# Shared expert of a fused recurrent and mixture-of-experts kernel: a PSUM copy on ScalarE ahead of an addition, and one operand sum formed earlier

## The chip, the cores and the metric

The kernel runs on one core of a Trainium2 chip. The metric is the device time of one execution in microseconds (us); before the change the median of three runs was 2733.51 us, from 2730.9 to 2735.72 us. Five engines work beside each other, each through its own queue in order: TensorE (PE, with its weight loads as PEld), VectorE (DVE), ScalarE (ACT), GpSimd (POOL) and SyncE (SP), which issues most of the DMAs.

## What is computed

Two layers act on `x` (128 sequences, 64 steps, 512 features, all float32). The reference, cut to its core:

```python
# layer 0: GRU over the 64 steps, a ternary-weight linear layer, residual
r = sigmoid(i_r + h_r); z = sigmoid(i_z + h_z); n = tanh(i_n + r * h_n)
h = (1 - z) * n + z * h
x = x + (hs @ ternary(weight).T + bias)
# layer 1: depthwise causal convolution, then a mixture of 64 experts (top 6) and a shared expert
hidden = conv(x, cond) + b
routed = combine(silu(buf @ w_gate) * (buf @ w_up) @ w_down)      # 64 slots an expert
shared = silu(hidden @ sw_gate) * (hidden @ sw_up) @ sw_down      # 512 -> 704 -> 512
x = x + routed + shared
```

The change lies in the shared expert alone: `silu(hidden @ sw_gate) * (hidden @ sw_up) @ sw_down` for all 8192 rows.

## The kernel before

The program has four stages, one after the other: the GRU with its input products and linear layer (to 1500 us), the convolution, a stage of shared expert blocks beside routing (from 1530 us), and a stage of shared expert blocks beside the routed experts (from 2084 us). The rows of the shared expert are cut into 16 blocks `i` of four steps (512 rows). `shared(i)` is a generator; after each of its `yield`s the caller may record a piece of routing (`route`), of slot counting (`count_slots`) or of an expert pair (`expert_pair`). The order that results is then rearranged within each engine by a scheduler when the program is built, so the order on an engine is read from the built program, not from the code.

**Gate and up part.** The 704 columns are five chunks of 128 (and a rest of 64, multiplied together at L818). Each chunk `c` is one `Block`: the two halves of the contraction and gate and up form a 2 by 2 block product that is done with seven products instead of eight (Strassen-Winograd). Each product is two matmuls of 128 x 256 at L644, and it adds into one of four PSUM tiles: products 1 and 2 into `psx`, 6 into `y`, 7 and 4 into `psw`, 5 and 3 into `psz`. They are recorded in the order 1, 6, 7, 3 of the chunk before, 2, 4, 5. Since products 4, 2 and 3 add onto what stands in the PSUM tile of 7, 1 and 5, the tile has to be read between the two:

- product 1 is copied by ScalarE into `u2` (L672), and product 6 is added to it (L674);
- product 7 is read by VectorE, `u3 = ps + u2` (L677), and only then may product 4 write `psw`;
- product 5 is read by VectorE, `aT = ps + u3` (L679), and only then may product 3 of the chunk write `psz`; L680 multiplies by the gate;
- product 2 goes through Silu on ScalarE into `g1` (L683), product 4 is added to `u2` and goes through Silu into `g2` (L686, L687), product 3 gives the other half of `aT` (L689, L690).

**Operand sums.** The products need sums of the rows: `s1`, `s2`, `s4` in `space` (L810, L811, L837) and a difference in place (L836). For blocks 0 and 1 `space` is a tile of its own; for blocks 2 to 7 it is the storage of the rows of block `i - 2` (L798), whose results leave by DMA at L911; from block 8 on it is the tile `es`, of which there is one. The scheduler places L810 and L811 of block `i + 2` where the storage of block `i`'s rows comes free, which for blocks 2 to 5 is among the instructions of block `i`'s second `Down`: L810 overwrites the first of the four rows, L811 the second, each once that row's DMA (L911) has read it.

**Down part.** From block 2 on (`PLAIN = 2`) the product with `sw_down` is done by `Down`, twice a block (`p` = 0, 1), again as seven products, in the order 6, 1 | 7, 5 | 2, 4, a piece `v` | 3, pieces x, w, z, then the rest at L771. `Down.__init__` forms sums of `aT` into places 6 and 7 of `space` (L723, L724) and a difference in place (L725). `last_sum` (L729 to L732) forms `s4 = x12 - s2` in a tile named `g1`, the name that the Silu of product 2 uses too. Product 1 is copied into `u2` (L740) and product 6 added (L741); product 7 is read by VectorE into `u3` (L744); product 5 is read by VectorE into `v` (L747), and only then may product 3 add into `psz`. L791 adds up the result rows, and L911 (GpSimd's queue) sends them with accumulation into the output. `u3` has one buffer, `u2` two.

The names of a profile's tiles leave buffer numbers out: `u2`, `u3` stand as `u`, `g1`, `g2` as `g`.

Of the kernel before, what the change touches and what calls it, by code (L numbers as in the profile page):

```python
# [8 lines left out]
F32 = mybir.dt.float32  # L9
# [10 lines left out]
P = 128  # L20
# [22 lines left out]
def adaln_ffn_kernel(  # L43
# [22 lines left out]
    nc = tc.nc  # L66
# [88 lines left out]
    def conv_group(sl, g, ps):  # L155

        ps = ps.rearrange("p (j h t) -> p j h t", j=4, h=2)
        for j in range(4):
            i = nc.tensor.matmul(  # L159
                ps[:, j],  # L160
                xcs[sl % 2][:, :, g * 4 + j],
                tzs[sl % 2][:, :, g * 4 + j, :],
                start=True,
                stop=True,
            )
        grouped.append(i)
        return ps
# [5 lines left out]
    HK = KD // 2  # L173
# [3 lines left out]
    with (  # L177
# [106 lines left out]
        class Chunk:  # L284


            def __init__(self, t, c, ops):
                self.c, self.ops, self.ws = c, ops, wsum[c]
                self.g = [gip.tile([P, 2, HD], F32, name="gi") for _ in range(2)]
                gis[t, c], gis[t + 1, c] = (g.rearrange("p h d -> p (h d)") for g in self.g)  # L290
                self.ps = {}
# [149 lines left out]
        for t in range(T):  # L441
# [9 lines left out]
            for c in (0, 2, 1):  # L451
                ps = ps_gh.tile([P, D], F32, name=f"psgh{c}")
# [60 lines left out]
    def hid(t):  # L513
        return hids[t // TH][:, t % TH, :]
# [20 lines left out]
    with tc.tile_pool(name="ps_c", bufs=4, space=PSUM) as ps_c:  # L535
        for sl in range(NSL):
# [7 lines left out]
            for g in range(DS // 4):  # L544
                if early:
                    ps = early.pop(0)
                else:
                    ps = conv_group(sl, g, ps_c.tile([P, D], F32, name="psc"))
# [27 lines left out]
    sh = ctx.enter_context(tc.tile_pool(name="sh", bufs=1, side="right"))  # L576
# [43 lines left out]
    QT = NB // 2 * P  # L620
# [9 lines left out]
    def winograd(n, accs, lhs, rhs, k0=0):  # L630


        name = {1: "x", 2: "x", 6: "y", 7: "w", 4: "w", 5: "z", 3: "z"}[n]
        first = n in (1, 6, 7, 5)
        if first:
            accs[name] = (
                ps_y.tile([P, D], F32, name="y")
                if n == 6
                else ps_gu.tile([P, D], F32, name=f"ps{name}")
            )[:, :QT]  # L640
        ps = accs[name]
        for k in range(HK):
            r = rhs(k)
            nc.tensor.matmul(  # L644
                ps.rearrange("p (j b) -> p j b", b=P) if len(r.shape) == 3 else ps,
                lhs(k),
                r,
                start=(first and k == 0),
                stop=(k == HK - 1),
                skip_group_check=not first,  # L650
            )
        return ps

    add, mul = nc.vector.tensor_add, nc.vector.tensor_mul

    class Block:
# [5 lines left out]
        def product(self, n):  # L662
            ps = winograd(
                n,
                self.accs,
                lambda k: sws[n][:, k, self.c * P : (self.c + 1) * P],
                lambda k: self.ops[n][:, k],
            )
            one, two = self.aT[:, :QT], self.aT[:, QT:]
            if n == 1:  # L670
                self.u2 = shu.tile([P, QT], F32, name="u2")
                nc.scalar.copy(self.u2, ps)  # L672
            elif n == 6:
                add(self.u2, self.u2, ps)  # L674
            elif n == 7:
                self.u3 = sh.tile([P, QT], F32, name="u3")
                add(self.u3, ps, self.u2)  # L677
            elif n == 5:
                add(two, ps, self.u3)  # L679
                mul(two, two, self.g2)  # L680
            elif n == 2:
                self.g1 = sh.tile([P, QT], F32, name="g1")
                nc.scalar.activation(self.g1, ps, AF.Silu)  # L683
            elif n == 4:
                self.g2 = sh.tile([P, QT], F32, name="g2")
                add(self.g2, ps, self.u2)  # L686
                nc.scalar.activation(self.g2, self.g2, AF.Silu)  # L687
            elif n == 3:
                add(one, ps, self.u2)  # L689
                mul(one, one, self.g1)  # L690
# [20 lines left out]
    class Down:  # L711


        def __init__(self, p, aT, aTr, space):
            self.p, self.aT, self.aTr, self.accs = p, aT, aTr, {}
            self.steps = [slice(p * QT + j * P, p * QT + (j + 1) * P) for j in range(2)]
            s1, s2 = (
                space[:, (6 + n) * QT : (7 + n) * QT].rearrange("p (k b) -> p k b", k=HK)
                for n in range(2)
            )  # L720
            x11, x12 = (aT[:, h_ * HK : (h_ + 1) * HK, self.steps[0]] for h_ in range(2))
            x21, x22 = (aT[:, h_ * HK : (h_ + 1) * HK, self.steps[1]] for h_ in range(2))
            add(s1, x21, x22)  # L723
            nc.vector.tensor_sub(s2, s1, x11)  # L724
            nc.vector.tensor_sub(x21, x11, x21)  # L725
            self.x12 = x12
            self.ops = {1: x11, 2: x12, 4: x22, 5: s1, 6: s2, 7: x21}

        def last_sum(self):  # L729
            s4 = sh.tile([P, QT], F32, name="g1").rearrange("p (k b) -> p k b", k=HK)  # L730
            nc.vector.tensor_sub(s4, self.x12, self.ops[6])
            self.ops[3] = s4  # L732

        def product(self, n):
            ps = winograd(
                n, self.accs, lambda k: self.ops[n][:, k], lambda k: sds[n][:, k]
            )
            if n == 1:
                self.u2 = shu.tile([P, QT], F32, name="u2")
                nc.scalar.copy(self.u2, ps)  # L740
                add(self.u2, self.u2, self.accs["y"])  # L741
            elif n == 7:
                self.u3 = sh.tile([P, QT], F32, name="u3")
                add(self.u3, ps, self.u2)  # L744
            elif n == 5:
                self.v = sh.tile([P, QT], F32, name="g2")
                add(self.v, ps, self.u3)  # L747
# [45 lines left out]
    def sums_space(i):  # L793

        if i < PLAIN:
            return sh.tile([P, 3 * D], F32, name="space")
        if i < NI // 2:
            return rows_of(i - 2).rearrange("p j d -> p (j d)")  # L798
        return esp.tile([P, 4 * D], F32, name="es")

    def shared(i, sums=None):
# [3 lines left out]
        x11, x12 = rows[:, :HK, :2], rows[:, HK:, :2]  # L805
        x21, x22 = rows[:, :HK, 2:], rows[:, HK:, 2:]
        space = sums_space(i)
        s = space[:, : 3 * D].rearrange("p (n k j b) -> p n k j b", n=3, k=HK, j=2)
        s1, s2, s4 = s[:, 0], s[:, 1], s[:, 2]
# [48 lines left out]
        if i < PLAIN:  # L858
            for p in range(2):
                ys = [  # L860
                    ps_y.tile([P, D], F32, name="y")
                    if p == 0
                    else ps_gu.tile([P, D], F32, name=f"ps{'wz'[j]}")
                    for j in range(2)
                ]
                for cs in (range(full - 1), range(full - 1, full)):
                    for j in range(2):
                        for c in cs:
                            nc.tensor.matmul(
                                ys[j],  # L870
                                aT[:, c, p * QT + j * P : p * QT + (j + 1) * P],
                                swd[:, c, :],
                                start=(c == 0),
                                stop=False,
                            )
                        yield
                for j in range(2):
                    part = slice(j * rest, (j + 1) * rest)
                    nc.tensor.matmul(ys[j], aTr[part, p], swdr[part], start=False, stop=True)
                for j in range(2):  # L880
                    nc.scalar.copy(hid(i * NB + 2 * p + j), ys[j])
        else:
            for p in range(2):
                down = after
                down.product(6)
                down.product(1)
                yield
                down.last_sum()
                down.product(7)
                down.product(5)  # L890
                yield
                down.product(2)
                down.product(4)
                down.block("v")
                if p == 0:
                    after = Down(1, aT, aTr, space)
                yield
                down.product(3)
                for name in ("x", "w", "z"):
                    down.block(name)  # L900
                down.finish(rows_of(i), sums)
                if sums is not None:
                    for t in range(i * NB + 2 * p, i * NB + 2 * p + 2):
                        nc.sync.dma_start(out=out_t[t], in_=sums[:, t % NB])
                yield
# [463 lines left out]
```

## Time and profile before

| what | value |
|---|---|
| median of three runs | 2733.51 us |
| profiled execution, whole | 2733.45 us |
| its span, first to last instruction | 2731.6 us |
| granted TensorE clock, mean | 0.997 |
| busy in the span: VectorE / ScalarE / GpSimd | 1413.4 / 426.1 / 425.6 us |
| copy of product 1 on ScalarE (L672), 80 of them | 372 ns each |
| addition of product 7 on VectorE (L677), 80 of them | 424 ns each |
| the same in the down part (L744), 28 of them | 424 ns each |
| last sum of the down part (L731), 28 of them | 393 to 426 ns each |

TensorE's rows count four matmul records for a product, two passes for each of its two matmuls. Idle time in brackets in a timeline is the idle time of that engine just before the instruction, with what ended it. [...]

### The profile page before, as it was taken

How to read it: one execution, taken by the hardware profiler on the slowest of the kernel's cores; microseconds unless marked ns; L12 is line 12 of the kernel's file. 1: busy time of each engine (PE TensorE's matmuls, PEld its weight loads, DVE VectorE, ACT ScalarE, POOL GpSimd, SP SyncE). 2: the span in 40 equal slices, each digit the busy share in tenths (PEclk: the TensorE clock that was granted, in tenths of full speed). 3: DMA queues.
4: the chain of work that ended last, by engine and by line, in shares of the span. 5: the costliest groups of instructions: out<-in, count | busy, mean ns of one | idle time of the engine just before them, and what ended most of it. 6: DMA issues, size and time to landing. Idle time of an engine off the chain costs nothing.

```text
span 2731.6 us, 30112 instructions
## 1 busy us (share of the span) xinstructions
PE 2704.8 (99%) x11447; PEld 1866.4 (68%) x11447; DVE 1413.4 (52%) x3143; ACT 426.1 (16%) x794; POOL 425.6 (16%) x471
## 2 busy tenths in 40 slices
PE   8999999999999999999999999999999999999999
PEld 5666666666666666666679766777876656666667
DVE  6555555555555555555554655555664333433334
ACT  1111111111111111111110222222221111111111
POOL 2111111121111112111010000000001222222120
PEclk9999999999999999999999999999999999999999
DMA  5333221121111112311157641122256898998962
GB/s 189 92 77 79 73 66 51 43 54 55 47 51 43 50 43 54 77 47 51 35 140 218 216 137 21 37 58 58 63 150 186 272 323 247 314 316 260 284 180 47
DMA packets 329360, 327.98 MB, mean 120 GB/s; under 512 B 184384, under 2 KB 250432, under 8 KB 327040
## 3 DMA queue, kind: packets, MB, share of 16 engines
q1 hardware_dynamic: 302672, 255.52, 30.7%
q0 software_dynamic: 25984, 66.86, 10.6%
q10 hardware_dynamic: 560, 3.67, 0.6%
q8 instruction: 91, 1.49, 0.2%
q14 instruction: 53, 0.43, 0.1%
HBM read 239.73 MB, written 94.65 MB: 122 GB/s over the span
## 4 chain that ended last, share of the span: by engine, by line
PE 95%; DMA 2%; issue 2%; DVE 1%; ACT 0%; SPq 0%; DVEq 0%; POOLq 0%; ACTq 0%
PE psgh L454 24%; PE psw L644 7%; PE psz L644 6%; PE psx L644 6%; PE psw L308 6%; PE psz L308 6%; PE psx L308 6%; PE psf L387 4%; PE psc L159 4%; PE py L1274 3%; PE y L644 3%; PE psy L308 3%; PE pg L1250 3%; PE pu L1250 3%; PE y L818 2%
## 5 line engine op out<-in xcount | busy, mean ns | idle before, releaser
L454 PE MATMUL psgh<-whh,hT 128*128 128x512 f32 x1536 | 676.3, 596 | 0.7 <-ACT hT L369 0.7
L454 PEld LDWEIGHTS psgh<-whh,hT 128*128 128x128 f32 x1536 | 287.2, 190 | 351.3 <-issue 337.2
L308 PE MATMUL psx<-wih,xp 128*128 128x256 f32 x768 | 198.5, 381 | 6.5 <-DMA wih<-in_w_ih_dram 6.0
L197 POOL DMA_DIRECT2D xn<-in_x_dram x61 | 33.9, 556 | 845.0 <-DVE x L395 833.4
L308 PEld LDWEIGHTS psx<-wih,xp 128*128 128x128 f32 x768 | 143.7, 191 | 25.8 <-issue 6.0
L464 DVE TENSOR_TENSOR n<-psgh,bhn 128x512 f32<-128x512 f32 x64 | 44.2, 691 | 175.3 <-PE psgh L454 175.3
L369 ACT COPY hT<-psf 128x512 f32<-128x512 f32 x64 | 37.4, 585 | 584.0 <-PE psf L363 584.0
L461 DVE TENSOR_TENSOR r<-psgh,gi 128x512 f32<-128x512 f32 x64 | 44.2, 691 | 143.3 <-PE psgh L454 143.3
L159 PE MATMUL psc<-tz,xc 128*128 128x128 f32 x480 | 105.7, 383 | 0.0
L159 PEld LDWEIGHTS psc<-tz,xc 128*128 128x128 f32 x480 | 105.6, 313 | 0.0
L383 POOL TENSOR_TENSOR xn<-xn,fb 128x512 f32<-128x512 f32 x64 | 80.7, 1262 | 155.3 <-DMA xn<-in_x_dram 155.3
L308 PE MATMUL psz<-wih,xs 128*128 128x256 f32 x384 | 98.7, 379 | 1.8 <-DVE gi L331 1.8
L308 PE MATMUL psy<-t,xs 128*128 128x256 f32 x384 | 99.9, 383 | 0.3 <-DVE t L259 0.2
L308 PE MATMUL psw<-t,xp 128*128 128x256 f32 x384 | 98.8, 380 | 0.4 <-DVE u L329 0.4
L308 PE MATMUL psw<-wih,xp 128*128 128x256 f32 x384 | 98.7, 379 | 0.0
L308 PE MATMUL psz<-t,xs 128*128 128x256 f32 x384 | 98.7, 379 | 0.0
L387 PE MATMUL psf<-sgn,hhi 128*128 128x512 f32 x256 | 95.1, 493 | 0.0
L1274 PE MATMUL py<-wd,aeT 128*64 128x512 f32 (+1 forms) x384 | 90.6, 601 | 0.0
L1259 DVE SCALAR_TENSOR_TENSOR a<-a,rw,pu 128x352 f32<-128x352 f32 x32 | 18.6, 580 | 136.8 <-PE pu L1250 122.4
L323 DVE TENSOR_TENSOR p<-psx,bi 128x512 f32<-128x512 f32 x96 | 66.3, 691 | 37.5 <-PE psx L308 37.2
L644 PE MATMUL psx<-xr,swg 128*128 128x256 f32 x320 | 84.3, 385 | 0.0
L1284 POOL DMA_INDIRECT out_dram<-ys,idxp x32 | 45.4, 1418 | 249.9 <-ACT ys L1282 200.1
(298 smaller groups left out, 4687.2 us busy)
## 6 DMA issues: line engine op xcount, KB each, us to landing
wg<-in_w_gate_dram SPq DMA_DIRECT2D x64, 704.0 KB
wu<-in_w_up_dram SPq DMA_DIRECT2D x64, 704.0 KB
wd<-in_w_down_dram SPq DMA_DIRECT2D x64, 512.0 KB
x1c<-x SPq DMA_DIRECT2D x62, 256.0 KB
out_dram<-x SPq DMA_DIRECT2D x62, 256.0 KB
xn<-in_x_dram POOLq DMA_DIRECT2D x61, 256.0 KB
xp<-in_xT_dram POOLq DMA_DIRECT2D x30, 512.0 KB
tab<-hid SPq DMA_DIRECT2D x60, 256.0 KB
```

Of the source, the lines that this page charges most:

```text
L159: i = nc.tensor.matmul(ps[:, j], xcs[sl % 2][:, :, g * 4 + j], tzs[sl % 2][:, :, g * 4 + j, :], start=True, stop=True,)
L308: i = nc.tensor.matmul(ps, self.ops[n][:, k, :], self.ws[n][:, k, :], start=(first and k == 0), stop=(k == HK - 1), skip_group_check=not f ...
L323: add(self.p1, both, b)
L383: nc.gpsimd.tensor_add(xn, xn, fb)
L387: nc.tensor.matmul(ps, piece[:, k, :], sgn[:, k, :], start=(i == 0 and k == 0), stop=(i == 1 and k == KD - 1),)
L454: nc.tensor.matmul(ps, hT[:, k, :], whh[c][:, k, :], start=(k == 0), stop=(k == KD - 1))
L461: nc.vector.tensor_add(r, ps_r, gis.pop((t, 0)))
L644: nc.tensor.matmul(ps.rearrange("p (j b) -> p j b", b=P) if len(r.shape) == 3 else ps, lhs(k), r, start=(first and k == 0), stop=(k == HK ...
L818: nc.tensor.matmul(gu.rearrange("p (j b) -> p j b", b=P), swr[:, k].rearrange("p w n -> p (w n)"), rows[:, k], start=(k == 0), stop=(k == ...
L1250: nc.tensor.matmul(acc[halves[j]], xeT[:, k, halves[j]], ws[j][which][:, k, :], start=(k == 0), stop=(k == KD - 1),)
L1274: nc.tensor.matmul(py[halves[j]], aeT[:n, c, halves[j]], ws[j][2][:n, c, :], start=(c == 0), stop=(c == len(ech) - 1),)
L1284: nc.gpsimd.indirect_dma_start(out=out, out_offset=bass.IndirectOffsetOnAxis(ap=(idxp[:CAP] if j == 0 else idxo)[:, q : q + 1], axis=0), i ...
```

## The change

Two things are changed. Product 7, in `Block` and in `Down`, is copied out of PSUM by ScalarE into `u3`, and VectorE then adds `u2` in place. And `Down` forms its last sum `s4` in its `__init__`, after the other three, in place `p` of `space` (the first two places, which held the row sums `s1`); the method `last_sum` and its tile named `g1` are gone.

```diff
             elif n == 7:
                 self.u3 = sh.tile([P, QT], F32, name="u3")
-                add(self.u3, ps, self.u2)
+                nc.scalar.copy(self.u3, ps)
+                add(self.u3, self.u3, self.u2)
...
             nc.vector.tensor_sub(x21, x11, x21)
-            self.x12 = x12
-            self.ops = {1: x11, 2: x12, 4: x22, 5: s1, 6: s2, 7: x21}
-
-        def last_sum(self):
-            s4 = sh.tile([P, QT], F32, name="g1").rearrange("p (k b) -> p k b", k=HK)
-            nc.vector.tensor_sub(s4, self.x12, self.ops[6])
-            self.ops[3] = s4
+            s4 = space[:, p * QT : (p + 1) * QT].rearrange("p (k b) -> p k b", k=HK)
+            nc.vector.tensor_sub(s4, x12, s2)
+            self.ops = {1: x11, 2: x12, 3: s4, 4: x22, 5: s1, 6: s2, 7: x21}
...
             elif n == 7:
                 self.u3 = sh.tile([P, QT], F32, name="u3")
-                add(self.u3, ps, self.u2)
+                nc.scalar.copy(self.u3, ps)
+                add(self.u3, self.u3, self.u2)
...
                 down.product(6)
                 down.product(1)
                 yield
-                down.last_sum()
                 down.product(7)
                 down.product(5)
```

## The prediction

> **What bounds the kernel now.** The page comes first: TensorE is busy for 99% of the span and makes up 95% of the chain that ended last, so an edit on VectorE or ScalarE counts only where TensorE waits for them.
>
> ```profile
> PE 2704.8 (99%) x11447; PEld 1866.4 (68%) x11447; DVE 1413.4 (52%) x3143; ACT 426.1 (16%) x794; POOL 425.6 (16%) x471
> PE 95%; DMA 2%; issue 2%; DVE 1%; ACT 0%; SPq 0%; DVEq 0%; POOLq 0%; ACTq 0%
> ```
>
> Second, TensorE's waits from 1530 us on, the stages with the shared expert (total, times, longest): 4.7 us for product 7's addition L677, which frees `psw`, and 1.2 us for L747, which frees `psz` in the down part.
>
> ```profile
> PE psw L644 <- DVE u L677: 4.7, 7, 0.8
> PE psz L644 <- DVE st L613: 1.4, 1, 1.4
> PE psz L644 <- DVE g L747: 1.2, 4, 0.4
> PE psz L644 <- DVE aT L689: 0.5, 1, 0.5
> ```
>
> Third, the timeline at one such wait, the first chunk of block 3. Product 7 was through by 1726.9, but L677 stood behind L837 (held by a DMA), L928, two pairs of L831 and L674, and ran at 1728.59. Product 4, due at 1727.22 + 4 x 0.216 = 1728.08, began at 1729.07: 0.99 us lost.
>
> ```profile
> 1725.28 0.38 ACT L829 ACTIVATE g<-y 64x256 f32<-64x256 f32 x1
> 1725.57 0.69 DVE L837 TENSOR_TENSOR hid<-hid 128x512 f32<-128x512 f32 x1 [2.64 <-DMA out_dram<-hid]
> 1725.68 0.37 ACT L672 COPY u<-psx 128x256 f32<-128x256 f32 x1
> 1725.92 1.03 PE L644 MATMUL psw<-hid,swu 128*128 128x256 f32 x4
> ...
> 1727.22 1.03 PE L644 MATMUL psx<-hid,swg 128*128 128x256 f32 x4
> ...
> 1727.56 0.38 ACT L829 ACTIVATE g<-y 64x256 f32<-64x256 f32 x1 [1.50 <-DVE aTr L831]
> ...
> 1728.59 0.42 DVE L677 TENSOR_TENSOR u<-psw,u 128x256 f32<-128x256 f32 x1
> ...
> 1729.07 0.48 PE L644 MATMUL psw<-hid,st 128*128 128x256 f32 x1 [0.82 <-DVE u L677]
> ```
>
> Fourth, VectorE at the end of block 2, the second `Down`. L810 waits for one output row's DMA, L747 follows it, L811 waits for the next row's.
>
> ```profile
> 1715.72 0.69 DVE L810 TENSOR_TENSOR hid<-hid 128x512 f32<-128x512 f32 x1 [1.72 <-DMA out_dram<-hid]
> 1716.33 0.42 DVE L747 TENSOR_TENSOR g<-psz,u 128x256 f32<-128x256 f32 x1
> 1717.87 0.69 DVE L811 TENSOR_TENSOR hid<-hid 128x512 f32<-128x512 f32 x1 [1.13 <-DMA out_dram<-hid]
> ```
>
> Both programs were also built and their order on each engine compared. TensorE keeps its instructions, with as many changes from one line to another (929) and nearly its order; VectorE keeps its counts; ScalarE gains 108 copies. VectorE's order changes in two repeated places, which decide the forecast (after's instructions under before's line numbers):
>
> ```
> end of blocks 2 to 5, before: L741, L744, L810, L747, L811, L791
> end of blocks 2 to 5, after:  L741, L810, L744, L811, L747, L791
> first Down of blocks 2 to 15: L731 before: after L690;  after: ahead of L679
> ```
>
> **Part 1, the copy on ScalarE.** 108 copies (80 + 28) at 372 ns (the rows of L672 and L740) are 40 us on an engine busy for 16%; VectorE's addition stays. What it can remove are the L677 waits. Counted like the 0.99 above they are 0.68 and 0.66 (blocks 1, 2), 0.99, 0.95, 0.89, 0.88 (blocks 3 to 6) and 0.85 (block 8): 5.9 us, the upper bound. The lower bound is 0, if the copy itself is late. In the built order the copy stands behind the second L829. In block 3 that starts at 1727.56; the copy follows 0.40 later (as L672 follows L829 at 1725.28 above), takes 0.37 and ends at 1728.33. With 0.05 for the release and 0.1 for a weight load no longer hidden (a group after a stall lasts 1.13 instead of 1.03) product 4 starts at 1728.48, so 0.6 of 0.99 is won; blocks 4 to 6 repeat it: 2.4. In blocks 1 and 2 L829 lies earlier (1603.41, copy done at 1604.18, product 4 due at 1604.24): all 1.34. In block 8 VectorE is held by gathered rows (L1235) on the next steps too, so I take 0.4 of 0.85. Together -4.1 us.
>
> `u3` has one buffer, so the copy now also waits for the previous chunk's L679. That ran at 1731.10 in block 3, and the next product 7 at 1733.07: covered. Behind the copy on ScalarE stand the two Silus, which wait for later products anyway.
>
> [...] This trace has 424 ns for L677, with a PSUM operand, and 425 ns for L690, with none. [...]
>
> **Part 2, the last sum earlier.** Removed is one instruction of 0.42 us after L690, where no wait of TensorE hangs on it. Added is the same one ahead of L679 in the first `Down` of 14 blocks, because its new place held `s1` and product 5 reads that last. L679 frees `psz` for product 3, and has little room:
>
> ```profile
> 2157.69 0.42 DVE L679 TENSOR_TENSOR aT<-psz,u 128x256 f32<-128x256 f32 x1
> ...
> 2158.25 1.05 PE L644 MATMUL psz<-es,swu 128*128 128x256 f32 x4
> ```
>
> Here (block 9) L679 would run from 2158.03 (+0.34, the distance of two such additions), end at 2158.45 and let product 3 start at 2158.60: 0.35 lost. The same sum gives 0.24 to 0.35 in blocks 7 to 12, 14 and 15 and nothing in 13 (a piece of expert work lies between): 2.3 us. In blocks 2 to 6 two instructions (L731, L959) now stand ahead, but one product matmul (0.43) was moved ahead of product 3: 0.15 each, 0.7. Sum +3.0; bounds 0 (if VectorE starts the sum earlier) and 14 x 0.35 = 4.9.
>
> From block 9 on the next block's L810 must wait for the second `Down`'s product 3, which now reads `es`. In block 8 that product ends at 2081.5; L810, L811 and L837, 0.72 apart as now, keep VectorE until 2083.6, and L791 behind them, which waits for TensorE's last matmuls, was due at 2083.5: almost hidden. I take +0.3 for all seven; without that cover 7 x 0.7 = 5.
>
> **Part 3, what both do to VectorE's order.** Now L747 stands behind L811. L811 cannot start before its DMA has landed, 1717.87 in block 2; L747 follows 0.61 later (L747 after L810 above), ends at 1718.90, and product 3 starts at 1718.95 instead of 1716.80: 2.15 us. Blocks 3, 4, 5, with L811 at 1779.83, 1841.02, 1903.06 and product 3 at 1778.49, 1840.30, 1901.84: 2.42, 1.80, 2.30. Sum +8.7. The DMA was issued after L791 of the first `Down`, before the stall, so its landing does not move; what follows (L791, the next rows' DMAs, L837) moves along with TensorE and gives nothing back. Bounds: 5.7 if that DMA landed 0.75 sooner each time, 11.7 if as much later.
>
> Block 0 has its sums L614 to L616 behind routing work; about 0.4 of new waits, from -0.3 to 1.
>
> **Sum.** -4.1 + 3.0 + 0.3 + 8.7 + 0.4 = +8.3 us on the profiled execution's 2733.45 (span 2731.6 and 1.85 around it; the median is 2733.51): 2741.8 us, 0.3% slower. No change means within 0.2%, 5.5 us, about what a measurement of this kernel can tell.
>
> **Rivals.** (a) Nearly balanced: the copy wins the whole 5.9, the early sum costs half, 1.5, and L811's DMA lands sooner: 2733.45 - 5.9 + 1.5 + 5.7 = 2734.8. For it: the L677 waits are there in every block. Against: the second L829 holds ScalarE. (b) Faster: L811's wait does not reach TensorE, because its DMA lands by 1715.9 instead of 1717.8, that is right after L810's row. This is one place, the second `Down` of blocks 2 to 5; from there on the copy's 4.1, plus the 1.9 of L747's present waits if L810 too comes early, stand against 3.7: 2731.2 us, and faster by over 5.5 needs the early sum hidden and the copy's whole 5.9 as well, 2726.4. Against: the two rows landed 1.8 to 2.4 us apart all four times. (c) Slower still: beside the experts the copy queues on ScalarE behind a copy of expert results (L1282) that waits for `py` or an output DMA; `psw` is then late where it never was. At 1 us for one chunk in five of 35, +7: 2749. For it: in the built order L1282 stands directly ahead of some copies, and waited 2.4 us for a DMA once. Against: TensorE's order puts those matmuls first too. (d) The change does not do what it says: excluded, the built order has the copies and the moved sum.
>
> **How the numbers follow.** Forecast 0.66, with its own range 2738 to 2746; (a) 0.17, (b) 0.06, (c) 0.11. Slower by over 0.2% (2739.0): 0.62 of the forecast and (c), 0.73. Within: the rest of the forecast, (a) and half of (b), 0.24. Faster: 0.03. The range reaches down into (a) and up to (c): 2735 to 2748.
>
> **What would show it.** In the profile after: L747 right behind L811 at the end of blocks 2 to 5, and TensorE's wait on L747 near 8 to 10 us instead of 1.2; the wait on L677 gone and one on the copy of some 1.5 us in its place; a wait on L679 of about 2 us in the later blocks. The forecast is wrong if L747's wait stays near 1 us, or if TensorE waits for ScalarE beside the experts.

## The result, and the profile after

The changed kernel takes 2743.21 us (median of six runs, 2741.28 to 2745.92) against 2731.86 us for the kernel before (six runs beside them, 2730.84 to 2735.72): a ratio of 1.0040, 95% interval 1.0027 to 1.0053. The profiled execution has a span of 2742.0 us, 10.4 more than the one of before.

Work moved as the code says. The page's first line of the changed kernel has 108 more instructions and 40 us more on ScalarE; VectorE has as many instructions as before (3143) and 1412.1 us instead of 1413.4:

```profile
PE 2708.1 (99%) x11447; PEld 1869.6 (68%) x11447; DVE 1412.1 (51%) x3143; ACT 466.4 (17%) x902; POOL 425.9 (16%) x471
```

Line numbers in the changed kernel: the copy of product 7 is L678 and its addition L679; product 5's addition L681; in the down part copy L743 and addition L744; the early sum L730; L747, L810, L811 are as before. TensorE's waits from 1530 us on (total, times, longest):

```profile
PE psz L644 <- DVE g L747: 9.7, 4, 2.5
PE psz L644 <- DVE st L613: 3.2, 1, 3.2
PE y L644 <- DVE es L726: 1.2, 1, 1.2
PE psz L644 <- DVE aT L691: 0.6, 1, 0.6
```

The line of L677 with 4.7 us is gone, the one of L747 has gone from 1.2 to 9.7 us, and no line names L681, the addition that the early sum stands ahead of. Counted as in the prediction (start of a matmul less the time it was due), L747 costs 10.39 us in four places instead of 1.89. The timeline at the first of them, the end of block 2:

```profile
1712.13 0.69 DVE L810 TENSOR_TENSOR hid<-hid 128x512 f32<-128x512 f32 x1 [2.40 <-DMA out_dram<-hid]
1712.15 0.59 PE L754 MATMUL y<-swd,aT 128*128 128x256 f32 x2
1712.74 0.42 DVE L744 TENSOR_TENSOR u<-u,u 128x256 f32<-128x256 f32 x1
1714.13 0.69 DVE L811 TENSOR_TENSOR hid<-hid 128x512 f32<-128x512 f32 x1 [0.98 <-DMA out_dram<-hid]
1714.74 0.42 DVE L747 TENSOR_TENSOR g<-psz,u 128x256 f32<-128x256 f32 x1
...
1715.21 2.07 PE L644 MATMUL psz<-swd,hid 128*128 128x256 f32 x4 [2.46 <-DVE g L747]
...
1717.08 1.06 PE L754 MATMUL psx<-swd,aT 128*128 128x256 f32 x2
```

L747 stands behind L811 and its DMA, as forecast. But the last two rows hold something that was not: the product takes 2.07 us instead of 1.03 and the piece behind it 1.06 instead of 0.59. The windows of the same stretch (busy time of PE, PEld, DVE, ACT, POOL with instructions, then the granted TensorE clock, DMA share and GB/s) show what goes with it:

```profile
1711.82:1715.23 3.41, 0.94 (x6) 0.49 (x4) 2.05 (x4) 0.00 (x0) 0.00 (x0) 1.00 0.38 65
1715.23:1718.64 3.41, 3.41 (x8) 2.78 (x9) 0.00 (x0) 0.00 (x0) 0.00 (x0) 0.50 0.00 0
1718.64:1722.05 3.41, 3.41 (x15) 1.80 (x15) 1.15 (x3) 0.37 (x1) 0.69 (x2) 1.00 0.00 0
```

After the stall the clock was granted at half for 3.41 us. The trace of the changed kernel has such a stretch of 3.41 us at 0.50 behind each of the four stalls (from 1715.23, 1780.08, 1844.93 and 1909.78 us) and one in block 8 (from 2073.63); the kernel before has none from 1532.97 us to its last microsecond. Measured from one L818 to the next, blocks 2 to 5 are 3.0 to 3.5 us longer each, block 8 is 1.4 longer, block 6 is 0.65 shorter, blocks 1 and 7 change by -0.5 and +0.2, and blocks 9 to 15 are the same to 0.01 us (the last to 0.11).

Two theories stood after this. A: the loss is the order of L811 and L747, plus a half-clock stretch behind each stall; the early sum is free. B: the prediction's sum, with the half clock unrelated to the stalls. It was also open which of the two edits brings the order.

### The profile page after: what moved, and what is told of

The parts are those of the page before. It is cut to its first block, busy times and chain, and to the rows that moved or that the text cites. A ratio compares the mean times of both kernels' runs of the same rounds, so it can differ in the third digit from the quotient of the medians.

```text
span 2742.0 us, 30320 instructions
## 1 busy us (share of the span) xinstructions
PE 2708.1 (99%) x11447; PEld 1869.6 (68%) x11447; DVE 1412.1 (51%) x3143; ACT 466.4 (17%) x902; POOL 425.9 (16%) x471
## 3 DMA queue, kind: packets, MB, share of 16 engines
q0 software_dynamic: 25984, 66.86, 10.4%
## 5 line engine op out<-in xcount | busy, mean ns | idle before, releaser
L467 ACT ACTIVATE n<-n 128x512 f32<-128x512 f32 x64 | 40.3, 629 | 274.0 <-DVE n L466 274.0
L644 PE MATMUL psx<-hid,swg 128*128 128x256 f32 x320 | 84.1, 385 | 0.7 <-ACT g L685 0.4
```

What stands on the lines that cost most here:

```text
L467: nc.scalar.activation(n, n, AF.Tanh)
L644: nc.tensor.matmul(ps.rearrange("p (j b) -> p j b", b=P) if len(r.shape) == 3 else ps, lhs(k), r, start=(first and k == 0), stop=(k == HK ...
```

## The experiments

Every kernel was timed in five rounds against the kernel before, whose medians in the three groups of runs were 2731.70, 2730.45 and 2730.66 us.

### One edit at a time

**The copy alone** (the kernel before with only the first hunks of the change).

> Kernel before with product 7 copied out by ScalarE in both classes; the down part's last sum stays after L690. VectorE's order at the end of blocks 2 to 5 is then that of the changed kernel: L741, L810, copy's addition, L811, L747, although the sum was not moved. Theory A (the copy alone brings the order; the stalls on L747 cost 8.5 us and each is followed by 3.41 us of TensorE at a granted clock of 0.5, some 1.65 us more): before 2731.9 - 4.7 (waits of product 7 gone) + 8.5 + 4 x 1.65 = 2742.3 us, wait on L747 near 10 us, four or more rows of clock 0.5. Rival B (the prediction's sum: no clock, the early sum costs 3): 2731.9 - 4.1 + 8.7 = 2736.5 us, and the missing rest with the sum. Rival C (the order comes from both edits together): 2731.9 - 4.5 = 2727.4 us, wait on L747 near 1.2 us.

Measured 2743.41 us, ratio 1.0036 (1.0023 to 1.0050): the whole loss without the moved sum. In its waits L747 is L749 (first line); the last of the four stalls is followed by half clock (0.50 from 1913.79 to 1917.20 us), and the mean granted clock is 0.996.

```profile
PE psz L644 <- DVE g L749: 9.9, 4, 3.3
```

**The early sum alone.**

```diff
 # changed kernel, in Block and in Down
-                nc.scalar.copy(self.u3, ps)
-                add(self.u3, self.u3, self.u2)
+                add(self.u3, ps, self.u2)
```

> Changed kernel with product 7's sum read from PSUM by VectorE again, as before; only the down part's last sum is early. VectorE's order at the end of blocks 2 to 5 is then that of the kernel before (L747 between L810 and L811). Theory A (the early sum takes the place of two copies of gathered rows, L1235, that go behind, and costs TensorE nothing in blocks 9 to 15; in block 8 the down part's sums wait for es, up to 1.2 + 1.65 us): 2731.9 + 0 to 3 us, 2732 to 2735, with blocks 9 to 15 as long as before to 0.1 us each. Rival B (the prediction: the early sum delays product 3 by 0.24 to 0.35 us in each late block, hidden in the changed kernel only because the copy made VectorE's product 7 work shorter): 2731.9 + 3.0 = 2735, spread over blocks 7 to 15.

Measured 2731.22 us, ratio 1.0001 (0.9992 to 1.0010); blocks 9 to 15 differ from before by no more than 0.05 us each, block 8 is 0.14 longer, and blocks 2 to 5 are 0.2 to 0.5 shorter (the waits on product 7's addition fell from 4.7 to 3.4 us; no run tells why). The sum costs nothing there with or without the copy, so rival B is out.

**The copy in the gate and up part only, and in the down part only.** Each has one of the two hunks with the copy.

> Kernel before with the copy on ScalarE in the 80 products of the gate and up part only; the down part keeps its addition from PSUM and its late sum. VectorE's order at the end of blocks 2 to 5 stays that of before (L810, L747, L811). Theory A (the waits of product 7 are all in the gate and up part; the loss comes with the down part's copy, which puts L744 one ScalarE step later and so lets L810 and L811 in ahead): 2731.9 - 4.7 = 2727.2 us, wait on L747 near 1.2 us. Rival B (the copy in either class moves the sums): 2737 us or more.

Measured 2727.00 us, ratio 0.9989 (0.9980 to 0.9998).

> Kernel before with the copy on ScalarE in the 28 products of the down part only. Theory A (the whole loss comes with this copy): VectorE's order at the end of blocks 2 to 5 is L741, L810, L744, L811, L747; the waits on L677 stay (5.9 us), the stalls on L747 rise by 8.5 us and bring four stretches of half clock: 2731.5 + 8.5 + 4 x 1.65 = 2746.6 us. Rival B (the order costs only together with the gate and up part's copy): 2732 us.

Measured 2747.07 us, ratio 1.0053 (1.0040 to 1.0067). Its waits show both the stalls on L747 (here L748) and the ones that the other copy would remove:

```profile
PE psz L644 <- DVE g L748: 10.1, 4, 3.2
PE psw L644 <- DVE u L677: 4.0, 7, 0.7
```

Its order at the end of block 2 is L741, L810, L744, L811, L747, that of the changed kernel; in the kernel with the 80 copies alone L744 and L747 stand where they stood before. Theory A had half clock behind all four stalls; the trace has 0.50 from 1853.06 to 1856.47 us, but 1.00 behind the last stall (the last section has the windows), and the five runs spread from 2742.5 to 2749.0 us, so that the hit on 2746.6 is no proof of the sum.

So 80 copies gain, and the 28 of the down part lose all that is lost. That they bring the order is shown by these two runs; the reason is argued from the code: they make L744 ready one ScalarE instruction later, and the order that is built for this has room for L810 and L811 ahead of L744 and L747.

### The order undone

```diff
 # changed kernel; v_sums keeps each L747, the addition of product 5 in Down
-        nc.vector.tensor_add(s1, x21, x22)
-        nc.vector.tensor_sub(s2, s1, x11)
+        held = 2 * PLAIN <= i < NI // 2
+        with tc.issue_after(v_sums[2 * (i - 2 - PLAIN) + 1].ins) if held else nullcontext():
+            nc.vector.tensor_add(s1, x21, x22)
+            nc.vector.tensor_sub(s2, s1, x11)
```

> Changed kernel, with the two sums L810 and L811 of the block after next put behind L747 in VectorE's queue (an issue order, four times); nothing else moves. Theory A (order plus clock): the stalls of 10.4 us on L747 go, and with them the four stretches of 3.41 us at clock 0.5: after 2743.2 - 10.4 - 6.6 = 2726 us, no granted clock under 1 in blocks 2 to 5. Rival B (the half clock is not tied to these stalls): 2743.2 - 10.4 = 2733 us, with four or five rows of clock 0.5 left between 1700 and 2080 us. Rival C (the sums are late where they now stand, and hold the next block's work): 2738 or more, with a wait of TensorE for L810 or L791 instead.

Measured 2726.15 us, ratio 0.9979 (0.9970 to 0.9989): 17.1 us less than the changed kernel, for four issue orders. The end of block 2 now (L747 is L748, L810 and L811 are L813 and L814):

```profile
1712.12 0.42 DVE L748 TENSOR_TENSOR g<-psz,u 128x256 f32<-128x256 f32 x1
...
1713.23 0.69 DVE L813 TENSOR_TENSOR hid<-hid 128x512 f32<-128x512 f32 x1 [0.69 <-DMA out_dram<-hid]
...
1714.00 1.03 PE L644 MATMUL psz<-swd,hid 128*128 128x256 f32 x4
...
1715.96 0.69 DVE L814 TENSOR_TENSOR hid<-hid 128x512 f32<-128x512 f32 x1 [2.04 <-DMA out_dram<-hid]
1716.25 0.48 PE L772 MATMUL psx<-swdr,aTr 64*128 64x256 f32 x1
```

L814 still waits for its DMA (2.04 us), but nothing that TensorE needs stands behind it: product 3 takes 1.03 us instead of 2.07. The mean granted clock is 0.999 instead of 0.997, which leaves room for two stretches of 3.41 us at half in the whole program, not for four (an estimate from mean and span: 2 x (1 - 0.9985) x 2724.2 = 8.2 us). Blocks 2 to 5 together are 18.5 us shorter than in the changed kernel's profile. The stalls were 10.4 of them. Half rate over 3.41 us, with TensorE busy for 3.41 of them (1715.23 to 1718.64 above), loses 1.7, and four such stretches 6.8; product 4 is late by 0.2 us there instead of 1.0, which is another 0.8; 0.5 stays unassigned. (The whole profiles differ by 17.8 us: block 8 is 1.3 shorter, about the 1.4 by which it had grown, and block 1 starts 2.1 later.)

> Copy on ScalarE alone, and L810, L811 behind L747 as in the run before this one; the last sum stays after L690. Theory A: before 2731.9 - 4.7 (product 7's waits) - 1.2 to 1.9 (what L747 waited for L810 before) = 2725 to 2726 us, faster than both kernels; if the early sum is free, within 2 us of the run with both edits and the order undone. Rival B (the copy only helps where something else stalls behind it): 2730 us or more.

Measured 2725.94 us, ratio 0.9980 (0.9970 to 0.9989), the same as with the early sum. Both versions beat both kernels, by 0.2% the kernel before.

### How long a stall brings the half clock

Two kernels were to make stalls of chosen length with additional VectorE instructions ahead of L747 (7 and 10 times, blocks 2 to 5).

```diff
             elif n == 5:
+                for _ in range(self.extra):
+                    nc.vector.tensor_tensor(self.u3, self.u3, self.u3, ALU.max)
                 self.v = sh.tile([P, QT], F32, name="g2")
```

> The copy kernel with L747's order undone (median 2725.9), and at the end of blocks 2 to 5 seven additional VectorE instructions on product 7's sum, each the maximum of it with itself, ahead of the addition of product 5. VectorE reaches that addition 7 x 0.40 - 1.5 (the time it had to spare in that place) = 1.3 us late, four times. [...] Rival B (any stall of over 1 us brings the half clock): 2725.9 + 4 x (1.3 + 1.65) = 2737.7 us, with four rows of 0.5.

Measured 2729.42 us, ratio 1.0001 (0.9991 to 1.0010).

> The same kernel with ten such instructions, so that the stall is 10 x 0.40 - 1.5 = 2.5 us, as long as those of the changed kernel, without any wait for a transfer and without the early sum. Theory A (idle length alone brings the half clock): 2725.9 + 4 x (2.5 + 1.65) = 2742.5 us with three or four stretches of 3.41 us at 0.5, each right behind a stall. Rival B (the half clock comes with the order of the two sums or with the transfers they wait for): 2725.9 + 4 x 2.5 = 2735.9 us and no row of 0.5 there.

Measured 2731.72 us, ratio 1.0005 (0.9996 to 1.0014). Neither tells anything of the clock, because the stalls did not come about: TensorE's order was built anew around the known VectorE work, with the next groups ahead of product 3. In the second of the two (L747 is L753) even the next block's L826 went ahead of it:

```profile
1716.03 0.59 PE L777 MATMUL psw<-swdr,aTr 64*128 64x256 f32 x2
1716.55 1.13 PE L826 MATMUL y<-hid,swr 128*128 128x512 f32 x2
1717.72 1.13 PE L644 MATMUL psz<-swd,g 128*128 128x256 f32 x4
```

TensorE waited 0.2 us here instead of 2.5. Blocks 2 to 6 together are still 4.0 and 5.3 us longer in these profiles than in the kernel that they started from; how much of that is the regrouped order was not settled. So these two runs leave open whether the half clock comes with the idle time or with the order of the sums and their transfers; the half clock that the kernel before has in its GRU stage, in the last section, speaks to that.

The third try used the real wait, a transfer: only L811 (here L814) is put behind L747 (L748), L810 (L812) stays ahead of L744 (L745).

> Changed kernel with only the second of the two sums, L811, put behind L747; L810 stays where it is, ahead of copy's addition L744. VectorE then waits for the first row's transfer alone, so L744 runs at the time it has in the changed kernel (1712.74 us in block 2) and L747 0.4 later: TensorE's stall is some 1.1 us instead of 2.6, four times. [...] Rival B (any stall of about 1 us brings 3.41 us of half clock): 2726.2 + 4 x (1.1 + 1.65) = 2737 us, with rows of 0.5 behind them.

Measured 2731.04 us, ratio 1.0004 (0.9995 to 1.0013); 2726.15 and four stalls of 1.1 us, without any half clock, make 2730.6. The end of block 2:

```profile
1713.62 0.69 DVE L812 TENSOR_TENSOR hid<-hid 128x512 f32<-128x512 f32 x1 [2.20 <-DMA out_dram<-hid]
...
1714.23 0.42 DVE L745 TENSOR_TENSOR u<-u,u 128x256 f32<-128x256 f32 x1
1714.75 0.42 DVE L748 TENSOR_TENSOR g<-psz,u 128x256 f32<-128x256 f32 x1
...
1715.23 1.13 PE L644 MATMUL psz<-swd,hid 128*128 128x256 f32 x4 [0.79 <-DVE g L748]
```

Its four stalls are 0.96, 1.41, 0.93 and 0.95 us, 4.25 in all; blocks 2 to 5 are 4.9 us longer than in the kernel without them (the medians, of two groups of runs, are 4.9 apart as well). The product behind the first stall takes 1.13 us, not 2.07, the clock behind the longest is 1.00, and the mean over the profile is 0.999. So these four cost 4.9 us for 4.25 us of stalls, while the four of the changed kernel cost their 10.39 us and, by the half clock, 6.8 more. The window with the longest of these stalls, and the one behind it:

```profile
1773.51:1776.92 3.41, 2.36 (x11) 1.72 (x10) 1.31 (x3) 0.00 (x0) 0.00 (x0) 1.00 0.75 119
1776.92:1780.33 3.41, 3.21 (x18) 2.50 (x18) 0.82 (x3) 0.12 (x1) 0.00 (x0) 1.00 0.00 0
```

### Why the early sum costs nothing

In block 10 before the change, product 5 and its addition L679:

```profile
2255.29 1.13 PE L644 MATMUL psz<-es,st 128*128 128x256 f32 x4
...
2256.46 0.42 DVE L679 TENSOR_TENSOR aT<-psz,u 128x256 f32<-128x256 f32 x1 [3.03 <-PE psz L644]
```

and the same place in the changed kernel:

```profile
2265.78 1.13 PE L644 MATMUL psz<-es,st 128*128 128x256 f32 x4
...
2266.52 0.43 DVE L730 TENSOR_TENSOR es<-aT,es 128x256 f32<-128x256 f32 x1 [2.60 <-PE psz L644]
...
2266.95 0.42 DVE L681 TENSOR_TENSOR aT<-psz,u 128x256 f32<-128x256 f32 x1
```

The addition starts 1.17 us after its product in both. L730 starts 0.74 us after it: its place is only the first half of `s1`, which the first of the product's two matmuls reads, and by the semaphores in the trace L730 waits for the end of that matmul (signalled at 2266.49 us) and L681 for the end of the second (2266.93). It runs while the second matmul does, in time in which VectorE waited. A kernel that takes this away: the early sum of the first `Down` goes to the second half of `s1` and is kept ahead of product 5's addition in the queue.

```diff
 # in the kernel with the order undone
-            s4 = space[:, p * QT : (p + 1) * QT].rearrange("p (k b) -> p k b", k=HK)
-            nc.vector.tensor_sub(s4, x12, s2)
+            s4 = space[:, (1 - p) * QT : (2 - p) * QT].rearrange("p (k b) -> p k b", k=HK)
+            self.last = nc.vector.tensor_sub(s4, x12, s2)
...
 # Block.product 5 of the last chunk; Down(0) is now formed between its matmuls and this addition
-                add(two, ps, self.u3)
+                with tc.issue_after(down.last.ins) if down else nullcontext():
+                    add(two, ps, self.u3)
```

> Changed kernel with L747 first (median 2726.2), with the early sum of the first Down written into the second half of s1 instead of the first, and kept ahead of product 5's addition in VectorE's queue. Product 5 reads the halves in turn, two matmul rows each; its second half is free only when the product ends. Theory A (the early sum cost nothing because the half that it overwrites is free 0.43 us before product 5 ends, as long as the sum takes): now the sum starts when the product ends, L679's addition 0.35 later, and product 3 is late by the 0.24 to 0.35 us that the prediction had, in most of blocks 7 to 15, and by up to 0.3 in blocks 2 to 6: 2726.2 + 2.3 to 4 = 2728.5 to 2730 us, with waits of TensorE for that addition of 2 to 4 us in all. Rival B (TensorE has room for a late product-5 addition whatever frees it): 2726.2 us and no such wait.

Measured 2724.59 us, ratio 0.9980 (0.9971 to 0.9989), not slower. In block 12 (the sum is L734, the addition L684):

```profile
2450.29 1.03 PE L644 MATMUL psz<-es,st 128*128 128x256 f32 x4
...
2451.36 0.43 DVE L734 TENSOR_TENSOR es<-aT,es 128x256 f32<-128x256 f32 x1 [0.44 <-PE psz L644]
...
2451.59 1.03 PE L644 MATMUL y<-space,es 128*128 128x256 f32 x4
2451.70 0.42 DVE L684 TENSOR_TENSOR aT<-psz,u 128x256 f32<-128x256 f32 x1
...
2452.46 1.03 PE L644 MATMUL psz<-es,swu 128*128 128x256 f32 x4
```

The half does what theory A says: the sum now waits for the whole product, and L684 starts 1.41 us after the product instead of 1.17 (0.34 behind the sum). But TensorE does not lose it: its order was built with all four matmul rows of the next product ahead of product 3, where two stood in the kernel that it starts from. No late block shows a new stall: the largest, 0.31 us in block 13, stands in the kernel before and in the changed kernel as well. So the expectation missed. The early sum is covered by the half that comes free early, and where that was taken away, by a TensorE order built around it; what a sum this late would cost under the old order stays open.

## Why the prediction came out where it did

The forecast was 2741.8 us, 8.3 over its profile; the profile went up by 10.4 and the median by 11.4. The direction and its main reason were right. That the number came within 1.4 us of the median is luck: the half clock, some 8.2 us, was missing, and against it stand 3.3 us for sums that cost nothing and a start that came 3.3 us earlier than reckoned.

| term, us | predicted | measured |
|---|---|---|
| copy, blocks 1 to 6 | -3.7 | -3.7 (5.04 of waits before, 1.33 after) |
| copy, block 8 | -0.4 | -0.1 to -0.3 (block 8 in the five kernels with the gate and up copy and the late sum) |
| early sum | +3.0 | 0, and 0.1 to 0.2 in block 8 |
| L810 waiting for `es` | +0.3 | 0 |
| L747 behind L811 | +8.7 | +8.5 |
| half clock | not in the sum | +6.8 in blocks 2 to 5 (half of four times 3.41), some 1.4 in block 8 |
| block 0 and all before it | +0.4 | -2.9 |

The measured terms add up to about 10 of the profile's 10.4 us; in blocks 2 to 5 alone, 8.5 of stalls, 6.8 of half clock and a gain of 2.5 by the copy make 12.8 of the 12.9 us there.

**The copy** was sized well as a sum. Product 4 is late by 0.17 to 0.28 us in each of blocks 1 to 6, 1.33 in all, where some 1.5 was forecast; the gain was smaller than reckoned in blocks 1 and 2 (0.9 of 1.34) and larger in 3 to 6 (2.8 against 2.4). In block 3 product 4 starts 0.26 us late instead of 0.99; the prediction had 0.4, with the copy behind the second L829, where it is:

```profile
1727.61 0.38 ACT L829 ACTIVATE g<-y 64x256 f32<-64x256 f32 x1 [1.46 <-DVE aTr L831]
1728.01 0.37 ACT L678 COPY u<-psw 128x256 f32<-128x256 f32 x1
...
1728.44 0.91 PE L644 MATMUL psw<-hid,st 128*128 128x256 f32 x3
```

In the kernel with the 80 copies alone and in the one with the order undone the six come to 0.4 us, so the copy can win 4.6 of the 5.04. In block 8 the wait changes its name: 0.85 on L677 goes, and the one on the down part's sums into `es` rises from 0.41 to 1.3.

**The early sum** is the step that failed in its mechanism: "because its new place held `s1` and product 5 reads that last". It holds for `s1` as a whole; the sum overwrites the half that is read first, and started 0.74 us after product 5 did, not at its end. The lower bound of 0 that the prediction named for "if VectorE starts the sum earlier" is what happened.

**The order.** The mechanism, the four places and the 8.7 us were right. The prediction laid it to both edits; it is the down part's copy alone. "Gives nothing back" was right as well: undoing it returned the stalls in full.

**The term that was missing** is the half clock. The profile of before had a sign: TensorE had 1.07 us of matmuls from 1389.61 to 1393.02 us, in the GRU stage, and the clock stood at 0.5 for the next 3.41. (Its other stretch, 10.24 us from 1522.73 us in the convolution, follows 2.48 us of matmuls in 3.41 and is no such plain case.) A sum made of stalls alone misses the 1.7 us by which each of the four stalls in blocks 2 to 5 was paid for again.

**Block 0 and before** went the other way, and no run ties that to an edit. The start of block 1 lies between 1592.5 and 1599.1 us in the twelve profiles of all kernels, without a pattern by edit that these runs could show: up to 1530 us the code is the same, half clock stands there and until 1532.97 us for 13.65 us in the profile of before (from 1393.02 and 1522.73 us) and for none in that of the changed kernel, and the wait of block 0 for L613, which reads `swu`, is 1.4 us before and 3.2 after, and 1.4 to 3.4 in the experiments, again without a pattern. Chance is the likely cause, not a shown one.

**Rivals.** (a) had the early sum at half its cost and the copy at the whole 5.9, but needed the transfer that L811 waits for to land sooner; the stalls on L747 came to 8.5 us, about the 8.7 of the forecast. (b) needed that too. (c) did not occur: from 2084 us on the changed kernel's profile has no wait of TensorE for ScalarE.

## What to carry to other kernels

Moving a PSUM read to another engine makes what follows it ready one instruction later (here a copy of 0.37 us); look in the built order for what that lets in ahead, above all an instruction that waits for a transfer, since the orders built here made room for additional VectorE instructions and not for that landing. Here four issue orders turned a change that lost 0.4% into one that gains 0.2%. And the in-place write here was released by the last reader of just the part that it overwrites (0.74 us after the product's start for the first half, 1.07 for the second), so the choice of the part is a choice of the time.

## What the runs showed of the hardware

In the changed kernel TensorE had 0.94, 1.14, 0.96 and 0.86 us of matmuls in the 3.41 us ahead of the half-clock stretches behind the four stalls on L747, and 1.66 ahead of the one in block 8; each stretch had 3.41 us at a granted clock of 0.50. The last stall of the copy-alone kernel, with 1.36 us of matmuls from 1910.38 to 1913.79 us, was followed by 0.50 as well. The kernel before was granted 0.50 for 10.24 us from 1522.73 us (2.48 us of matmuls in the 3.41 us ahead) and for 3.41 us from 1393.02 us (1.07), in the GRU stage, where the two sums and the transfers they wait for do not run: the half clock came without them too. What separates a stall with half clock behind it from one without was not shown. The down-part copy's last stall kept the full clock with 1.51 us of matmuls in 3.41 (first two lines), while block 8 of the changed kernel got half with 1.66 (last two):

```profile
1914.51:1917.92 3.41, 1.51 (x7) 0.97 (x6) 1.97 (x4) 0.00 (x0) 0.00 (x0) 1.00 0.46 75
1917.92:1921.33 3.41, 3.27 (x18) 2.50 (x18) 0.22 (x2) 0.18 (x1) 0.00 (x0) 1.00 0.00 0
```

```profile
2070.22:2073.63 3.41, 1.66 (x7) 0.81 (x5) 2.61 (x10) 0.38 (x1) 0.00 (x1) 1.00 0.45 150
2073.63:2077.04 3.41, 3.37 (x8) 2.71 (x9) 1.75 (x5) 0.42 (x1) 0.00 (x0) 0.50 0.00 0
```

The copy kernel with the order undone has the same two waits in its view as the changed kernel in block 8 (0.6 us on the second half of `aT`, 1.2 on the sum into `es`), and its profile has a mean clock of 1.000; one stretch of 3.41 us at half in its span of 2721.4 us would make it 0.999. The same pair of waits thus came once with half clock behind it and once without, and no run tells why.
